# Attention and quantized feed-forward on one core: later reciprocals' halves, mixed pieces kept as integers, a calendar of weight jobs

## The chip, the cores and the metric

One Trainium2 chip, one of its cores. The metric is device time in microseconds of one launch; the time shown is the median of three runs. The profile is of one execution of the program.

Engines by the profile's names: PE (matrix products), PEld (its loading of the stationary operand), DVE (vector engine), ACT (scalar engine), POOL, and SP, whose queue (SPq) issues nearly all transfers. Each engine and SP's queue work through their own instructions in order; semaphores make one wait for another.

## The reference

All of it is in fp32: x is 16 x 512 x 512 (16 batch elements of 512 tokens), the context 16 x 120 x 512.

```python
x = x + attention(layernorm(x), ctx, ctx, Wq, Wk, Wv, Wo)    # 16 heads of 32, rotary positions on q and k
h = act_qdq(layernorm(x))
up   = act_qdq(h @ lpbq_dequant(w_up).T)       # 512 -> 1536
gate = act_qdq(h @ lpbq_dequant(w_gate).T)
gate = act_qdq(gate * u16(sigmoid(gate)))
x = x + act_qdq(gate * up) @ lpbq_dequant(w_down).T
```

`act_qdq` rounds a whole tensor to 16 bits with one scale, the tensor's largest absolute value over 32767. So gate, its product with the sigmoid, up, and the last product each need a maximum over all 16 elements before any of their values can be quantized. `lpbq_dequant` rounds weights to 4 bits in blocks of 32.

## The kernel before

Tokens are handled one batch element after another; a step of 512 tokens is one column block of PE. There are four stages.

**Attention** (L176 to L660). For each element `b` a loop runs over four slots `g` = 0 to 3, each with four heads. While element `b` is here, element `b+1` (`nxt`) has its queries made, `b-1` (`old`) is divided by its sums, projected and added to x, and `b-2` (`older`) is normalized and its largest absolute value found. A slot holds, in this order: scores of PE; DVE's maxima over keys (L335), turned by PE (L347, tile `tm`) and made into negated maxima `nm` (L354); the rotation of new queries on DVE (L217, L219) and POOL; values and sums of the slot before; exponentials. In slot 0 `old.reciprocals` makes 1/sum on DVE (L394), a copy to fp32r on ACT (L488), and then on DVE, in place, the lower halves of half the rows (L489, `two_halves`), which the copy must precede. The copy's tile `rh` shares its buffer with a raw weight, so it also waits for that weight's store. In slot 1 `old.divide` spreads the reciprocals over the heads by a matmul (L400, `rp`) and multiplies (L404). Three PSUM banks of tag `w` serve `qp`, `tm`, `pv`, `rp`, `op` and the rest in turn. In elements with `b % 4` in 1 to 3, up to 11, the slots 0 and 1 also hold parts of the next group's keys (`kvs.go_on`); elements 4, 8 and 12 to 15 have none.

**Gate** (L765 to L963). Tokens are quantized to int16, transposed by a DMA, and split into fp32r pieces: `hi` by POOL or DVE (L732), `lo` (L735) and `mix` = hi - 4096 lo by DVE (L738). An element has six chunks `f`, each two blocks of 128 gate columns; chunk `i` runs in `step(i)`: the mixed products of chunk `i+1` (`begin`, 8 matmuls), ACT's copy of chunk `i-1` out of PSUM and its store, ACT's division of `i+1` (L802), then the rest of `i` (16 matmuls). Then DVE finds the largest values of chunk `i-1` (L819, twice). Element `b+1` is quantized in the first step of `b` (third step for the first) and its pieces are made in steps 1 to 4. The same loop prepares the other weights: a block is loaded, quantized on DVE, turned by PE through two banks, cut into three parts and stored. Twelve blocks of up start at elements 1 to 12 and take one job per step; four blocks of down start in step 4 of elements 2, 5, 8 and 11, their six jobs one per step, beside those of up.

**Up** (L967 to L1155). The same steps with up's weights, elements 15 and 14 first (their pieces are still there), the others from their stored int16 tokens (`xq_d`, fetched into `xq`, two buffers). In each step a gate tile is loaded (`gt<-g_d`, seven buffers), turned by ACT (L980, L986) and DVE (L990, L991) into its product with the sigmoid, stored (`p_d<-gt`), and multiplied by up on POOL (L1014) for the largest product (L1018). Up itself is stored too (`u_d<-t_wu`, three buffers).

**Down** (L1157 to the end). The products are quantized, split and multiplied by down's weights.

PE, DVE and ACT, and in gate and up POOL too, follow the order of the code; SP's order is made by the scheduler of the language from its own estimate of when things are ready.

Of the kernel before, what the change touches and what calls it, by code (L numbers as in the profile page):

```python
# [53 lines left out]
def tile_xattn_ffn(  # L54
# [41 lines left out]
    xq_d = [dram.tile([P, NQ, ND, P], I16, name=f"xq_{b}") for b in range(B)]  # L96

# [84 lines left out]
    with ExitStack() as at:  # L182
# [92 lines left out]
        class Element:  # L275
# [66 lines left out]
            def maxima(self, g):  # L342
# [9 lines left out]
                hl = two_halves(p2.tile([P, DK], F32R, tag="mh", name=f"mh_{nm}"), mx, low_m)  # L352
# [36 lines left out]
            def reciprocals(self, part=slice(0, S)):  # L389
# [5 lines left out]
                two_halves(self.rh[:, part], self.rc[:, part], low_r, nc.scalar.copy)  # L395
# [90 lines left out]
        def two_halves(hl, t, low, copy=nc.vector.tensor_copy):  # L486

            copy(hl, t)  # L488
            nc.vector.scalar_tensor_tensor(  # L489
                out=hl, in0=hl.bitcast(F32), scalar=low, in1=t, op0=ALU.mult, op1=ALU.add  # L490
            )
            return hl
# [62 lines left out]
        for b in range(B):  # L555
# [8 lines left out]
            for g in range(NG):  # L564
# [13 lines left out]
                here.maxima(g)  # L578
                for f in rest:
                    f()  # L580
# [13 lines left out]
                if older and g in (1, 2):  # L594
                    for q in ((1,), (2, 3))[g - 1]:
# [43 lines left out]
        last.reciprocals(halves[0])  # L639
        for g in range(NG):  # L640
            last.divide(g, halves[0])
        last.reciprocals(halves[1])
        rest = last.output(0)
# [90 lines left out]
    def split_low(p, q):  # L734
        nc.vector.tensor_tensor(  # L735
            as_runs(p.lo, q), q, as_runs(p.hi, q).bitcast(F32), ALU.subtract
        )
        nc.vector.scalar_tensor_tensor(  # L738
# [27 lines left out]
    with ExitStack() as gu:  # L766
# [5 lines left out]
        class Tokens:  # L772


            def __init__(self, b, nm):
                self.b, self.nm, self.p = b, f"{nm}_{b}", []
                self.q = xpool.tile([P, NQ, ND, P], I16, tag="xq", name=f"xq_{self.nm}", bufs=2)
# [5 lines left out]
            def low(self, d):  # L783
                split_low(self.p[d], self.q[:, :, d, :])
# [67 lines left out]
        def quantize(b):  # L852
# [6 lines left out]
            nc.sync.dma_start(xq_d[b], xs[b].q)  # L859
# [64 lines left out]
        ups, downs = [], []  # L924
        for b in range(B):
            for f in range(N2):
                i = b * N2 + f

                def middle():
                    if f == (0 if b else 2) and b + 1 < B:  # L930
                        quantize(b + 1)

                def after():

                    if b == 0:
                        high = {3: ((0, nc.vector), (1, nc.gpsimd), (2, nc.gpsimd)), 4: ((3, nc.vector),)}
                        low = {3: (0,), 4: (1, 2, 3)}
# [492 lines left out]
```

## Time and profile before

| | us |
|---|---|
| median of three runs (range) | 2675.11 (2673.24 to 2676.17) |
| profiled execution: time / span | 2674.77 / 2673.0 |
| PE busy, share of the span | 2518.4, 94% |
| DVE / POOL / ACT busy | 2107.2 / 1598.2 / 1101.5 |
| mean granted clock of PE | 0.976 |
| HBM traffic over the span | 178 GB/s |

Attention lasts to 954 us, gate to 1526, up to 2080, and down begins at 2118 (its first matmuls) and runs undisturbed from 2148. The page's slices show PE near full everywhere but at the changes of stage; what PE loses inside a stage is in short gaps, which only its timeline shows. In a timeline row the columns are the start, the length, engine, line, operation with its tiles, and in brackets the idle time before it and what ended that.

### The profile page before, as it was taken

The numbers are of one execution on the slowest core, as the hardware profiler recorded it, in microseconds if no ns is written. First come the engines' busy times: TensorE is split into PE (matmuls) and PEld (weight loads), VectorE is DVE, ScalarE is ACT, GpSimd is POOL, SyncE is SP. The second block draws the span as 40 slices with busy tenths as digits, with TensorE's granted clock in tenths as the row PEclk, the third lists the DMA queues.
The fourth block names the chain that finished last, engine by engine and source line by source line (L and its number), as shares of the span: only waits on it lengthen the run. The fifth ranks groups of instructions, "written<-read, shape, count | busy, mean of one in ns | idle before, by whom it ended". The sixth has DMA issues, their size and how long they took to land. (4 is left out here: it accounts for less than half of the span.)

```text
span 2673.0 us, 30019 instructions
## 1 busy us (share of the span) xinstructions
PE 2518.4 (94%) x10610; PEld 1674.4 (63%) x10610; DVE 2107.2 (79%) x2889; ACT 1101.5 (41%) x1199; POOL 1598.2 (60%) x1011
## 2 busy tenths in 40 slices
PE   8899999999999779999999999999999489999999
PEld 4344334344333258778787878877777368888887
DVE  4677877887787657887886589999998778888886
ACT  1222222232222224444444377776667344444442
POOL 4467656565754345555554157776665467777775
PEclk9999999999999889999999999999999699999999
DMA  4011221121110076766665788888888877777774
GB/s 157 19 63 48 75 78 48 52 75 51 59 57 24 24 267 201 224 201 205 218 192 178 270 289 286 282 286 270 285 278 282 333 252 252 252 252 252 252 252 142
DMA packets 264399, 486.83 MB, mean 182 GB/s; under 512 B 47024, under 2 KB 65584, under 8 KB 264240
## 3 DMA queue, kind: packets, MB, share of 16 engines
q1 hardware_dynamic: 264080, 484.31, 53.4%
q8 instruction: 84, 1.38, 0.2%
q14 instruction: 75, 0.61, 0.1%
q0 software_dynamic: 160, 0.52, 0.0%
HBM read 255.66 MB, written 221.25 MB: 178 GB/s over the span
## 5 line engine op out<-in xcount | busy, mean ns | idle before, releaser
L732 POOL TENSOR_SCALAR oh_d<-oq_d 128x512 fp32r<-128x512 int16 x190 | 398.9, 2121 | 153.1 <-DVE oq_d L1220 153.1
L1014 POOL TENSOR_TENSOR po<-gt,t_wu 128x1024 f32<-128x1024 f32 x96 | 231.5, 2411 | 241.9 <-DVE gt L991 145.1
L308 PE MATMUL qp<-xnT,wq_sb 128*128 128x512 f32 x512 | 237.6, 607 | 2.3 <-ACT cT L204 2.3
L410 PE MATMUL op<-wo_sb,ao 128*128 128x512 f32 x512 | 233.9, 605 | 0.2 <-DVE ao L404 0.2
L387 ACT COPY ao<-pv 128x512 f32<-128x512 f32 x64 | 37.5, 586 | 467.8 <-PE pv L378 467.8
L819 DVE TENSOR_REDUCE max_g<-t_wg 128x1 f32<-128x1024 f32 x96 | 116.7, 1216 | 133.5 <-ACT t_wg L814 133.5
L732 POOL TENSOR_SCALAR xh_g<-xq_g 128x512 fp32r<-128x512 int16 x60 | 122.3, 2058 | 163.5 <-DMA xq_g<-xi 157.7
L796 PE MATMUL mm_wg<-xm_g,wg 128*128 128x512 f32 x768 | 202.5, 406 | 9.4 <-DMA wg<-wg_d 4.6
L1237 PE MATMUL dn_d<-wd,om_d 128*128 128x512 f32 x768 | 194.7, 403 | 17.6 <-DMA wd<-wd_d 6.4
L752 PE MATMUL mm_wg<-xl_g,wg 128*128 128x512 f32 x768 | 207.5, 392 | 0.0
L752 PE MATMUL mm_wg<-xh_g,wg 128*128 128x512 f32 x768 | 206.2, 390 | 0.0
L220 POOL TENSOR_TENSOR rt_q<-rt_q,sin_q 128x512 f32<-128x512 f32 x64 | 81.3, 1270 | 192.9 <-DVE rt_q L217 192.9
L1220 DVE SCALAR_TENSOR_TENSOR oq_d<-pq_d,r_o,uq_d 128x1024 int16<-128x1024 int16 x96 | 127.5, 1328 | 82.1 <-ACT uq_d L1173 82.1
L752 PE MATMUL mm_wu<-xl_u,wu 128*128 128x512 f32 x672 | 184.7, 397 | 2.1 <-ACT mm_wu L802 2.1
L1237 PE MATMUL dn_d<-wd,ol_d 128*128 128x512 f32 x768 | 184.6, 389 | 0.4 <-ACT dn_d L1249 0.4
L796 PE MATMUL mm_wu<-xm_u,wu 128*128 128x512 f32 x672 | 172.6, 397 | 12.7 <-ACT t_wu L814 6.5
L1237 PE MATMUL dn_d<-wd,oh_d 128*128 128x512 f32 x768 | 184.5, 389 | 0.0
L1237 PEld LDWEIGHTS dn_d<-wd,om_d 128*128 128x128 f32 x768 | 144.9, 192 | 62.2 <-DVE om_d L738 18.9
L752 PE MATMUL mm_wu<-xh_u,wu 128*128 128x512 f32 x672 | 180.0, 390 | 0.0
L308 PEld LDWEIGHTS qp<-xnT,wq_sb 128*128 128x128 f32 x512 | 92.6, 190 | 133.7 <-issue 104.6
L796 PEld LDWEIGHTS mm_wg<-xm_g,wg 128*128 128x128 f32 x768 | 147.8, 196 | 43.0 <-DVE xm_g L738 8.5
L814 ACT COPY t_wg<-mm_wg 128x1024 f32<-128x1024 f32 x96 | 97.2, 1012 | 173.5 <-PE mm_wg L752 138.3
(254 smaller groups left out, 5602.1 us busy)
## 6 DMA issues: line engine op xcount, KB each, us to landing
g_d<-t_wg SPq DMA_DIRECT2D x96, 512.0 KB, 3.7
gt<-g_d SPq DMA_DIRECT2D x96, 512.0 KB, 4.6
u_d<-t_wu SPq DMA_DIRECT2D x96, 512.0 KB, 5.8
p_d<-gt SPq DMA_DIRECT2D x96, 512.0 KB, 5.1
p<-p_d SPq DMA_DIRECT2D x96, 512.0 KB, 4.8
u<-u_d SPq DMA_DIRECT2D x96, 512.0 KB, 5.8
xt<-in_x_dram SPq DMA_DIRECT2D x16, 1024.0 KB, 5.3
x<-xt SPq DMA_DIRECT2D x16, 1024.0 KB, 4.3
```

Of the source, the lines that this page charges most:

```text
L220: nc.gpsimd.tensor_tensor(v(t), v(t), sin, ALU.mult)
L308: nc.tensor.matmul(ps, lhsT=wq_sb[:, d, ts(g, P)], rhs=self.xnT[:, d, :], start=(d == 0), stop=(d == ND - 1),)
L387: nc.scalar.copy(self.ao[:, g, :], pv)
L410: nc.tensor.matmul(ps, lhsT=self.ao[:, g, ts(q, P)], rhs=wo_sb[:, g, :], start=(g == 0), stop=(g == NG - 1),)
L732: engine.tensor_scalar(as_runs(p.hi, q), q, TO_256, TO_256, ALU.add, ALU.subtract)
L752: nc.tensor.matmul(ps[:, j, :], lhsT=lhs(j, i)[k], rhs=rhs(j, i)[k], start=(k == 0 and i == 0), stop=(k != 1 and i == n - 1), skip_group_c ...
L796: nc.tensor.matmul(self.ps[:, j, :], lhsT=lhs(j, d), rhs=self.x.p[d].mix, start=(d == 0), stop=(d == ND - 1), skip_group_check=True,)
L814: nc.scalar.copy(self.t, halves(self.ps))
L819: nc.vector.tensor_reduce(maxes[:, i : i + 1], self.t, AX.XYZ, ALU.max, **how)
L1014: nc.gpsimd.tensor_tensor(flat(g.po), flat(g.tile), flat(c.t), ALU.mult)
L1220: nc.vector.scalar_tensor_tensor(out=oq.rearrange("p f t -> p (f t)"), in0=pq, scalar=r_o, in1=uq, op0=ALU.mult, op1=ALU.mult,)
L1237: nc.tensor.matmul(self.ps[j], lhsT=self.p[f // 2].all()[k][:, f % 2, ts(j, P)], rhs=wd.made[f][k], start=(k == 0 and f == 0), stop=(k != ...
```

## The change

Five edits. (1) The lower halves of the reciprocals become a step of their own (`lower_reciprocals`), called in slot 1 after the maxima of the next element's scores; the quotients of the first two head groups move ahead of the key work of slot 1, the other two stay behind it; the three remaining maxima of normalized rows all stand in slot 2. (2) In gate the mixed pieces of elements 0 to 13 are turned into int16 by ACT (they are multiples of 256) in steps 2 and 3 and stored in `xn_d`. In up they are fetched beside the tokens, and ACT makes the fp32r piece again; DVE's L738 is left out there. The token tiles `xq` have one buffer rather than two; the store of tokens is a job of its own (`keep`) and left out for elements 14 and 15. (3) The weight jobs follow a calendar by step number. (4) The second element is quantized in step 1 of the first, and its lower pieces are made in pairs. (5) The scale of the largest gate is found at step 2 of up instead of 3. The first number after a job's start in the calendar is a step of the block's element, counted from 0; for down, 4 is the fifth step of its element and 7 to 10 are steps 1 to 4 of the next.

```diff
...
+    xn_d = [dram.tile([P, ND, S], I16, name=f"xn_{b}") for b in range(B)]
...
                 nc.vector.reciprocal(self.rc[:, part], self.sm[:, part])
-                two_halves(self.rh[:, part], self.rc[:, part], low_r, nc.scalar.copy)
+                nc.scalar.copy(self.rh[:, part], self.rc[:, part])
+            def lower_reciprocals(self, part=slice(0, S)):
+                lower_half(self.rh[:, part], self.rc[:, part], low_r)
...
-        def two_halves(hl, t, low, copy=nc.vector.tensor_copy):
-
-            copy(hl, t)
+        def lower_half(hl, t, low):
             nc.vector.scalar_tensor_tensor(
                 out=hl, in0=hl.bitcast(F32), scalar=low, in1=t, op0=ALU.mult, op1=ALU.add
             )
-            return hl
...
                 here.maxima(g)
+                if g == 1 and old:
+                    old.lower_reciprocals()
                 for f in rest:
                     f()
...
                     older.largest(0)
                     older.end_normalize(3)
-                if older and g in (1, 2):
-                    for q in ((1,), (2, 3))[g - 1]:
+                if older and g == 2:
+                    for q in range(1, NQ):
                         older.largest(q)
                 if new and g == 2:
                     for q in range(NQ):
...
                         old.reciprocals()
                     if nxt:
                         nxt.query(1)()
+                if g == 1 and old:
+                    for i in range(2):
+                        old.divide(i)
                 if g < 2 and kvs:
                     kvs.go_on(2)
                 if g == 1 and old:
-                    for i in range(NG):
+                    for i in range(2, NG):
                         old.divide(i)
                 if g == 2 and old:
                     for q in range(2):
...
         engine.tensor_scalar(as_runs(p.hi, q), q, TO_256, TO_256, ALU.add, ALU.subtract)
-    def split_low(p, q):
+    def split_low(p, q, mix=True):
         nc.vector.tensor_tensor(
             as_runs(p.lo, q), q, as_runs(p.hi, q).bitcast(F32), ALU.subtract
         )
+        if mix:
+            split_mix(p)
+    def split_mix(p):
         nc.vector.scalar_tensor_tensor(
             out=p.mix, in0=p.lo.bitcast(F32), scalar=-SPLIT, in1=p.hi.bitcast(F32),
...
             def __init__(self, b, nm):
                 self.b, self.nm, self.p = b, f"{nm}_{b}", []
-                self.q = xpool.tile([P, NQ, ND, P], I16, tag="xq", name=f"xq_{self.nm}", bufs=2)
+                self.q = xpool.tile([P, NQ, ND, P], I16, tag="xq", name=f"xq_{self.nm}", bufs=1)
             def high(self, d, engine):
                 self.p.append(Pieces(xpool, "x", [P, S], 8, f"{self.nm}_{d}"))
                 split_high(self.p[d], self.q[:, :, d, :], engine)
-            def low(self, d):
-                split_low(self.p[d], self.q[:, :, d, :])
+            def low(self, d, mix=True):
+                split_low(self.p[d], self.q[:, :, d, :], mix)
+            def keep(self):
+                nc.sync.dma_start(xq_d[self.b], self.q)
+            def short_mixes(self, pool, ds):
+                if ds[0] == 0:
+                    self.n = pool.tile([P, ND, S], I16, tag="xn", name=f"xn_{self.nm}", bufs=1)
+                for d in ds:
+                    nc.scalar.mul(self.n[:, d, :], self.p[d].mix.bitcast(F32), 1.0 / 256.0)
+                if ds[-1] == ND - 1:
+                    nc.sync.dma_start(xn_d[self.b], self.n)
+            def fetch(self):
+                nc.sync.dma_start(self.q, xq_d[self.b])
+                self.n = xpool.tile([P, ND, S], I16, tag="xn", name=f"xn_{self.nm}", bufs=1)
+                nc.sync.dma_start(self.n, xn_d[self.b])
+            def mix(self, d):
+                nc.scalar.mul(self.p[d].mix, self.n[:, d, :], 256.0)
         class Chunk:
             def __init__(self, w, x, b, f):
...
                 xi, xs[b].x1.rearrange("p q d -> p (q d)"), AF.Copy, scale=r_x
             )
             nc.sync.dma_start_transpose(xs[b].q.rearrange("p q d t -> p (q d) t"), xi)
-            nc.sync.dma_start(xq_d[b], xs[b].q)
         def up_weight(o):
...
         for d in range(ND):
             xs[0].high(d, nc.vector if d < 2 else nc.gpsimd)
             xs[0].low(d)
+        xs[0].keep()
         load(1)
         normalize(1)
         wg.load(range(4, NF))
-        nc.sync.dma_start(xq_d[0], xs[0].q)
         nc.vector.tensor_scalar(s_xw, s_x, WHOLE, None, ALU.mult)
         order = [B - 1, B - 2, *range(B - 2)]
...
         chunks[0].x = xs[0]
         chunks[0].begin()
         chunks[0].divide()
-        ups, downs = [], []
+        jobs = {}
+        for o in range(NF):
+            start = (o + 1) * N2
+            when = ((1, 2, 4, 5), (0, 1, 3, 4), (0, 1, 4, 5))[o % 3]
+            for j, job in zip(when, up_weight(o)):
+                jobs.setdefault(start + j, []).append(job)
+        for o in range(ND):
+            start = (3 * o + 2) * N2
+            for j, job in zip((4, 5, 7, 8, 9, 10), down_weight(o)):
+                jobs.setdefault(start + j, []).insert(0, job)
         for b in range(B):
             for f in range(N2):
                 i = b * N2 + f
                 def middle():
-                    if f == (0 if b else 2) and b + 1 < B:
+                    if f == (0 if b else 1) and b + 1 < B:
                         quantize(b + 1)
+                    if f in (2, 3) and b < B - 2:
+                        xs[b].short_mixes(wp, ((0, 1), (2, 3))[f - 2])
                 def after():
                     if b == 0:
                         high = {3: ((0, nc.vector), (1, nc.gpsimd), (2, nc.gpsimd)), 4: ((3, nc.vector),)}
-                        low = {3: (0,), 4: (1, 2, 3)}
+                        low = {3: (0, 1), 4: (2, 3)}
                     else:
                         high = {k: ((2 * k - 2, nc.gpsimd), (2 * k - 1, nc.gpsimd)) for k in (1, 2)}
                         low = {2: (0, 1), 3: (2,), 4: (3,)}
...
                     if i > 0:
                         chunks[i - 1].largest(max_g, **size)
                         chunks[i - 1].largest(top_g)
+                    for job in jobs.pop(i, ()):
+                        job()
+                    if f == 2 and b + 1 < B - 2:
+                        xs[b + 1].keep()
                     if f == 2 and b + 2 < B:
                         load(b + 2)
                     if f == 4 and b + 2 < B:
                         normalize(b + 2)
-                    if f == 0 and 1 <= b <= NF:
-                        ups.extend(up_weight(b - 1))
-                    if f == 4 and b % 3 == 2 and b < NF:
-                        downs.extend(down_weight(b // 3))
-                    for jobs in (downs, ups):
-                        if jobs:
-                            jobs.pop(0)()
                     if b == B - 1:
                         wu.load((0,) if f == 0 else (2 * f - 1, 2 * f))
...
             def middle():
                 for j in sig[k]:
                     gates[j].sigmoid2()
+                if splits:
+                    xu[order[n + 1]].mix(f)
             def after():
                 if k == 0:
                     wu.load((NF - 1,))
                 if splits:
-                    xu[order[n + 1]].low(f)
+                    xu[order[n + 1]].low(f, False)
                 if n + 2 < B and f == ND:
                     b = order[n + 2]
                     xu[b] = Tokens(b, "u")
-                    nc.sync.dma_start(xu[b].q, xq_d[b])
+                    xu[b].fetch()
                 if n == B - 1:
                     wd.load((0,) if f == 0 else range(max(1, 2 * f - 3), 2 * f - 1), (0,))
...
                 m_g = over_all([max_g, top_g], "g")
                 s_g, r_g = scale_of(m_g[:, 0:1], s_xw, "g")
                 nc.vector.tensor_tensor(r_g, r_g, s_xw, ALU.mult)
-            if k == 3:
+            if k == 2:
                 nc.vector.tensor_copy(m_p, m_g[:, 1:2])
...
```

More of the change, by code (lines that the diff above doesn't have):

```diff
@@ L351, in maxima @@
                 )
-                hl = two_halves(p2.tile([P, DK], F32R, tag="mh", name=f"mh_{nm}"), mx, low_m)
+                hl = p2.tile([P, DK], F32R, tag="mh", name=f"mh_{nm}")
+                nc.vector.tensor_copy(hl, mx)
+                lower_half(hl, mx, low_m)
                 t = p2.tile([P, NB, DK], F32R, tag="nm", name=f"nm_{nm}", bufs=1)
@@ L639, in tile_xattn_ffn @@
         last.reciprocals(halves[0])
+        last.lower_reciprocals(halves[0])
         for g in range(NG):
@@ L642, in tile_xattn_ffn @@
         last.reciprocals(halves[1])
+        last.lower_reciprocals(halves[1])
         rest = last.output(0)
```

## The prediction

> **What bounds the kernel now.** I read the page first (busy shares, then the slices), then busy time by stage, then PE's own timeline with the gaps in it, and for each gap the timeline of the engine or queue that ended it. The profiled execution took 2674.77 us (span 2673.0 and 1.8 around it); the median of the three runs is 2675.11, so a sum made on this execution stands 0.3 us below it.
>
> Busy time by stage (columns: stretch, its length, PE, PEld, DVE, ACT, POOL, granted clock, DMA share, GB/s); the rows are attention, gate, up in two parts, the change-over, and down:
>
> ```profile
> 0.00:954.00 954.00, 888.09 (x3593) 363.53 (x3593) 706.53 (x1329) 233.85 (x323) 539.68 (x523) 0.98 0.18 61
> 954.00:1526.00 572.00, 551.12 (x2410) 452.54 (x2411) 417.90 (x465) 236.22 (x232) 285.54 (x144) 0.97 0.68 218
> 1526.00:1755.00 229.00, 223.37 (x979) 182.71 (x978) 212.01 (x218) 163.26 (x162) 150.91 (x62) 1.00 0.85 286
> 1755.00:2080.00 325.00, 315.14 (x1320) 241.17 (x1319) 300.17 (x290) 224.64 (x223) 213.99 (x89) 1.00 0.84 284
> 2080.00:2148.00 68.00, 24.98 (x86) 18.19 (x85) 44.95 (x76) 20.97 (x22) 31.15 (x15) 0.66 0.76 283
> 2148.00:2673.00 525.00, 515.72 (x2229) 416.22 (x2227) 425.60 (x514) 222.51 (x241) 376.94 (x180) 1.00 0.69 242
> ```
>
> PE leads in every stage, so the change is worth what it takes out of PE's gaps, and no more. On PE's timeline an undisturbed chunk of gate or up takes 5.44 us from start to start, so an element of six takes 32.64. Three kinds of gap matter.
>
> Attention, element 4, slot 1, both counted from 0 (timelines of DVE, PE): DVE idles 1.85 us for ACT's copy of the upper halves, then makes the lower ones, and the transposed maxima reach PE 2.42 us late.
>
> ```profile
> 280.23 3.34 DVE L394 RECIPROCAL rc<-sm 128x512 f32<-128x512 f32 x1
> 285.42 0.75 DVE L489 SCALAR_TENSOR_TENSOR rh<-rh,low_r,rc 128x512 fp32r<-128x512 f32 x1 [1.85 <-ACT rh L488]
> 287.31 2.37 DVE L335 TRANSPOSE_TENSOR_REDUCE mt<-st 128x32 f32<-128x1024 f32 x2
> 289.97 0.33 PE L347 MATMUL tm<-ident,mt 128*128 128x128 f32 x1 [2.42 <-DVE mt L340]
> ```
>
> Gate, element 3: the up weight is transposed in the step that also turns the third part of a down weight. The two banks are full, and PE waits until DVE has read the second part:
>
> ```profile
> 1088.13 0.69 DVE L169 TENSOR_TENSOR wt_wd<-tp_wd,wt_wd 128x512 f32<-128x512 f32 x1
> 1088.92 1.09 PE L159 MATMUL tp_wu<-ident,wt_wu 128*128 128x128 f32 x4 [3.73 <-issue]
> ```
>
> Up (waits of SP's queue, then its timeline, then issues with time to landing and DVE's groups, all between 1820 and 2050): each load of a gate tile waits until the store of the previous tenant of its buffer, issued just before, has landed. Store, landing, load, next store: the stores of products go out every 5.88 us (69 of them from 1665.9 to 2071.7), slower than 5.44.
>
> ```profile
> SPq L1002 <- DMA p_d<-gt: 143.9, 39, 4.8
> ...
> 1908.05 0.57 SPq L1002 DMA_DIRECT2D gt<-g_d  x1
> 1908.71 0.56 SPq L1009 DMA_DIRECT2D p_d<-gt  x1
> 1909.32 0.62 SPq L815 DMA_DIRECT2D u_d<-t_wu  x1
> 1913.92 0.57 SPq L1002 DMA_DIRECT2D gt<-g_d  x1
> ...
> p_d<-gt SPq DMA_DIRECT2D x39, 512.0 KB, 5.2
> ...
> L738 DVE SCALAR_TENSOR_TENSOR xm_u<-xl_u,xh_u 128x512 fp32r<-128x512 f32 x25 | 22.2, 888 | 0.9
> ```
>
> **The change, part by part.**
>
> *Lower halves, maxima, quotients (attention).* DVE in slot 0 loses 0.75 and the wait of 1.85, together 2.60. The same gap of 2.41 to 2.42 stands in elements 4, 8, 12 and 13 (289.97, 512.84, 735.48, 786.46), all without key work, with 1.42 in 14 (835.98). In 15 (881.10) the gap is 3.82, of which a wait of 0.69 and the 0.75 vanish, less 0.3 until the scores end: 1.1. Sum 4 x 2.42 + 1.42 + 1.1 = 12.2. The granted clock fell to half for 3.4 us at 736.7 and 787.9, right behind two of these gaps: 1.7 each, 3.4. Against it: in slot 1 the 0.75 now stands between the negated maxima and the rotation. PE ends the exponents' matmuls 0.66 after DVE's nm (380.23 to 380.89), the lower halves come after 0.75 + 0.22 of signal: 0.3 for the first quotient in 14 elements, 4. The quotient gaps now present (16, 11.5 in all) are bank waits; with two quotients ahead of the key work some go, and the later rotation makes others: I count 2 gained. The maxima (0.68 each) move from slot 1 to 2, where DVE idles 0.70 for an output matmul (421.33). Net 14; bounds 8 (no clock, no bank wait gained) and 18.
>
> Rule weighed: the Trainium skill, "TensorE: Matmul & The Clock Gate", part 1, has the clock fall after an idle window of about 3.4 us. Of four stalls of 2.42 us here two were followed by half clock; by the page's figure none need be, and the sum would be 3.4 less.
>
> *Calendar of weight jobs (gate).* Elements 3, 6, 9 and 12 take 39.74, 41.29, 40.21 and 40.46 us, the others with a weight 33.1 (32.64 and 0.46 for four transposes). Twelve more transposes cost 3 x 0.46, so 34.5 is their floor: 161.7 - 138.0 = 23.7. In the calendar no step turns both weights, and the down weight's first turn comes two steps after its quantization (6.9 on DVE, 1065.4 to 1072.3) rather than one. DVE's fullest step is step 2: lower halves and mixes 2.8, two maxima 2.4, rest of a turn 1.4, 6.6 in 5.44; a bank is needed again one step after. I take 22; bounds 15 (a stall of 2 left in each) and 24.
>
> *Mixed pieces as integers, write side.* Four ACT conversions in each of 14 elements, two in step 2 and two in step 3 (all steps counted from 0): bounded by the 0.62 of ACT's fp32r cast and the 0.71 of its int16 output from 128x512. ACT is busy 41% in gate, two conversions are 1.4 beside 2.0 of a step's own: hidden by that idle time. One store of 512 KB per element at 218 GB/s: hidden, since 354 GB/s is seen elsewhere (2050 to 2110); if not, a landing of 3.7 (the row of g_d) each, off PE's path. On SP it waits for ACT's last conversion and stands before a store of gate that ACT has yet to make; the tokens' own store, now its own job, is put by the scheduler where it was.
>
> *First tokens.* Stall before element 1: 2.74 + 0.96, and 6.8 us of half clock. The quantization one step earlier does little: SP issues 24 weight loads until 974.3, the transposition went out at 976.8 and can go about 1.4 sooner. 1.4; bounds 0 and 6.
>
> *Up, the mix on ACT.* DVE per element: six times 0.72 + 1.28 + 1.21 + 1.21 is 26.5, four lower halves of 1.02 are 4.1, four mixes of 0.89 are 3.6: 34.2 before, 30.6 after, against 32.64. ACT's step is 1.02 + 1.15 + 1.01 + 1.14 = 4.32 of 5.44; with 0.62 in four of six steps 4.94, so PE covers it with 0.5 to spare. What is late next is SP. The built order of the changed kernel has, per element, only four loads with no later product store between them and the one they wait for (six before); the other two stand behind a later one, and the two token fetches between stores without a load. Four cycles of 5.88 and about 5.9 for the two other steps are 29.4, under 32.64. Bytes: 20 transfers of 512 KB in 32.64 us are 321 GB/s against 279 now and 354 seen. From the start of element 2 (1587.1) to PE's last up matmul (2080.5) 493.4 us pass; 85 steps of 5.44 are 462.4. Of 31 I take 28, leaving 0.2 an element; bounds 5 (SP still at 5.88 from element 8 on) and 31.
>
> *One buffer of tokens instead of two.* A fetch now waits for the last reader of the buffer, the fourth lower half, in step 3; it goes out in step 4 and lands in 6.5, and POOL reads it at the next element's first step, 10.9 later. The product store behind it on SP waits for a later DVE operation anyway. Cost 0; if that cover is gone, up to 6.5 in each of 14. Rule weighed: the Trainium skill, "Trainium Kernel Development and Optimization", Best Practices, wants double buffering so that transfers overlap compute, which speaks against this edit; with every landing exposed the sum would be 91 worse. The two steps of distance in the order decide for me.
>
> *Scale of the largest gate a step earlier:* some ten DVE operations of 0.15 to 0.2, moved, not added: 0, at most 2 either way.
>
> *Change-over.* The last store of up went out at 2088.3, 7.8 after PE's last matmul, behind SP's lag and full output buffers. Without the lag up to 8 go; the loads of down weights and DVE's chain of small operations to 2112.9 stay. I take 4; bounds 0 and 8.
>
> Sum: 14 + 22 + 1.4 + 28 + 4 = 69.4, so 2674.8 - 69.4 = 2605.
>
> **Rivals.** *Up stays on SP's queue.* For: 512 KB more per element, and landings of products grew from 3.3 to 5.2 as traffic ran on; from 6.0 on the four cycles and the rest fill 32.64. Against: the order above. Gains lost 28 - 5 and about 3 of the change-over: 2631.
> *ACT becomes up's bound.* If each mix shows in full, 56 x 0.62 = 35, 2640. For: ACT works in order and its copies already waited 69 us for stores. Against: 0.5 spare a step.
> *The attention edit does nothing,* because the moved 0.75 is paid again in slot 1: 2619.
> *Slower.* The single token buffer holds the transposition in gate: an ordinary element's last mix is ready at 1058.3, PE wants it at 1061.8, so 3.5 of delay is free and the rest falls on PE. To pass 2675 all 14 elements must lose 5.0, a transposition 8.5 late each time. Against: its last reader is done two steps ahead.
>
> **How the numbers follow.** All parts work: 0.69, 2605, own range 2594 to 2618. Up on SP: 0.13. Attention nothing: 0.09. ACT: 0.05. Slower: 0.04. The range 2590 to 2633 takes in the first three. About 0.2% (5.3 us) is what a measurement can tell from no change; between the cases and that bound lies little: faster 0.95, same 0.01, slower 0.04.
>
> **What would show it.** Right: no idle at the transposed maxima in elements 4, 8, 12, 13; gate elements 3, 6, 9, 12 near 34.5; up elements near 32.7 to the end; product stores following their DVE operation within 3 us rather than 11.8. Wrong: SP's wait for landed products still near 3.7 a step, ACT rows in front of up's divisions, or POOL idle at the tokens' upper halves for longer than before.

## The result and the profile after

The changed kernel takes 2638.31 us (median of four, 2635.48 to 2643.51) against 2675.64 for the kernel before: ratio 0.9864, 95% interval 0.9846 to 0.9881. It is faster, by half of what was forecast: 37 us instead of 69, and above the range of 2590 to 2633.

Its profiled execution took 2643.51 (span 2641.7). Busy time by stage, the columns as before; the rows are attention, gate, and up in two parts:

```profile
0.00:946.00 946.00, 888.27 (x3593) 361.56 (x3593) 717.11 (x1329) 234.18 (x323) 538.79 (x523) 0.98 0.18 61
946.00:1516.00 570.00, 551.87 (x2408) 450.17 (x2409) 416.30 (x465) 262.74 (x287) 278.58 (x145) 0.97 0.71 230
1516.00:1745.00 229.00, 228.38 (x1009) 188.81 (x1008) 209.41 (x206) 182.51 (x193) 152.15 (x64) 1.00 0.91 316
1745.00:2049.00 304.00, 299.98 (x1290) 238.73 (x1289) 281.55 (x246) 233.35 (x248) 199.36 (x86) 1.00 0.88 306
```

PE's share of attention and of up's first part has grown. Gate's row has hardly changed: 551.87 of 570 us busy, where it was 551.12 of 572. For exact borders I take PE's own marks: the first mixed matmul of gate, the first of up, the last matmul of up, the first of down.

| us | before | after | gained | forecast |
|---|---|---|---|---|
| attention, to gate's first matmul | 954.4 | 946.7 | 7.7 | 14 |
| gate | 565.8 | 564.0 | 1.8 | 23.4 (22 and 1.4) |
| up | 560.3 | 539.3 | 21.0 | 28 |
| change-over | 37.4 | 36.9 | 0.5 | 4 |
| down | 555.1 | 554.9 | 0.2 | 0 |

The profiled execution was the slowest of the four. Most of the experiments below leave some stages as they are here. Over the profiles with the same work in a stage, attention ends at 945.7 on average (14 profiles, 940.8 to 949.8; with the old attention 954.1 in three), gate takes 561.7 (6, 560.4 to 564.0) and up 536.0 (9, 531.0 to 539.6). By these averages the gains are 8.4, 4.1 and 24.3, the 37 us of the medians.

**Attention**, the same slot of element 4, PE and DVE. The wait for ACT's copy is gone, and the 2.42 us in front of `tm` are down to 0.39. In their place PE waits 0.17 for the negated maxima and 0.43 for a bank that the rotation frees, now that the lower halves stand in front of the rotation:

```profile
285.71 3.35 DVE L397 RECIPROCAL rc<-sm 128x512 f32<-128x512 f32 x1
290.21 2.37 DVE L336 TRANSPOSE_TENSOR_REDUCE mt<-st 128x32 f32<-128x1024 f32 x2
295.64 0.74 DVE L494 SCALAR_TENSOR_TENSOR rh<-rh,low_r,rc 128x512 fp32r<-128x512 f32 x1
...
293.43 0.33 PE L348 MATMUL tm<-ident,mt 128*128 128x128 f32 x1 [0.39 <-DVE mt L341]
295.78 0.51 PE L365 MATMUL st<-nm,ones 32*128 32x512 f32 x4 [0.17 <-DVE nm L357]
297.67 1.09 PE L406 MATMUL rp<-rh,rep 128*128 128x512 f32 x2 [0.43 <-DVE ra_q L220]
```

**Gate.** The collision is gone: elements 3, 6, 9, 12 take 34.49, 34.38, 34.50, 34.38, within 0.2 of the forecast floor of 34.5, and the 15.8 us that PE spent at `tp_wu` are down to 1.8. But elements 5, 8, 11 and 14, which took 33.1 and 32.6, now take 38.48, 38.48, 39.62 and 34.85. PE's waits from 946 to 1510:

```profile
PE mm_wg L832 <- DVE xm_g L753: 15.1, 10, 2.8
PE mm_wg L832 <- DMA wg<-wg_d: 5.0, 2, 4.6
PE tp_wu L160 <- DVE wt_wu L152: 1.8, 3, 1.0
```

One such stall, ahead of element 5 and followed back through the timelines of PE, SP and POOL (element 4 starts its own work at 1094.3):

```profile
1127.54 0.73 PE L832 MATMUL mm_wg<-xm_g,wg 128*128 128x512 f32 x2 [2.85 <-DVE xm_g L753]
...
1103.01 0.32 SPq L898 DMA_DIRECT2D wu_d<-wa_wu  x1
...
1105.85 0.34 SPq L135 DMA_DIRECT2D wt_wu<-in_L_ffn_w_up_dram  x1
1106.28 3.01 SPq L894 DMA_TRANSPOSE xq_g<-xi  x1
...
1092.18 1.29 POOL L172 TENSOR_TENSOR wa_wd<-wt_wd,wt_wd 128x512 f32<-128x512 f32 x1 [3.59 <-ACT wt_wd L171]
1093.46 8.27 POOL L883 TENSOR_SCALAR x1t<-x1t,ln_mv,ln_rstd 128x512 f32<-128x512 f32 x4
```

Read from the bottom: the calendar puts the rest of the down weight's third turn into step 4, in front of the normalization of the tokens two elements on. POOL idles 3.59 us for it, then normalizes for 8.27. Only then can ACT quantize (it ends 9.5 after the element's start; before, 5.0), and only behind the up weight's stores and load does SP issue the transposition (12.0; before, 5.0). The fourth mix of the next tokens is ready at 33.2, where before it was at 24.9; PE begins with these tokens at 28.3 and stands for that mix from 30.4. Small losses stand beside this one in elements 4, 7 and 10 (33.9, 33.6 and 34.4, before 33.1).

**Up.** Counted from 0 in the order of up, all chunks of elements 1 to 9 take 5.44; from 10 on they take 5.4 to 6.8, because the old wait is back. SP's waits from 1820 to 2050 (us in all, times, longest), its timeline around a pair of token fetches (a row `x2` is two loads and the wait between them), the issues with their time to landing, and ACT's new group (busy time, mean ns of one, idle time in front); the last two are from 1820 to 2050 again:

```profile
SPq L1047 <- DMA p_d<-gt: 123.2, 35, 6.0
```

```profile
1737.22 0.55 SPq L1054 DMA_DIRECT2D p_d<-gt  x1
...
1738.75 1.03 SPq L815 DMA_DIRECT2D xq_u<-xq  x1
1739.88 1.05 SPq L817 DMA_DIRECT2D xn_u<-xn  x1
1741.02 0.55 SPq L1054 DMA_DIRECT2D p_d<-gt  x1
...
1743.26 0.97 SPq L1054 DMA_DIRECT2D p_d<-gt  x1
...
1747.94 5.54 SPq L1047 DMA_DIRECT2D gt<-g_d  x2
1753.58 0.56 SPq L1054 DMA_DIRECT2D p_d<-gt  x1
```

```profile
p_d<-gt SPq DMA_DIRECT2D x42, 512.0 KB, 5.3
```

```profile
L820 ACT ACTIVATE xm_u<-xn_u 128x512 fp32r<-128x512 int16 x23 | 14.2, 618 | 0.0
```

ACT's mix costs the 0.62 that was assumed, with no idle time in front. SP still stands 3.5 us at each of 35 loads, and product stores go out up to 12 us after the start of the DVE operation they follow.

### The profile page after: what moved, and what is told of

Read it like the earlier page. It is cut to its first block, busy times and chain, and to the rows that moved or that the text cites. A ratio compares the mean times of both kernels' runs of the same rounds, so it can differ in the third digit from the quotient of the medians.

```text
span 2641.7 us, 30187 instructions
## 1 busy us (share of the span) xinstructions
PE 2510.0 (95%) x10610; PEld 1674.0 (63%) x10610; DVE 2095.2 (79%) x2833; ACT 1155.9 (44%) x1311; POOL 1577.0 (60%) x1011
## 5 line engine op out<-in xcount | busy, mean ns | idle before, releaser
L336 DVE TRANSPOSE_TENSOR_REDUCE mt<-st 128x32 f32<-128x1024 f32 x128 | 151.7, 1223 | 30.2 <-PE st L330 29.9
```

The costliest lines, as they stand in the source:

```text
L336: nc.vector.tensor_reduce(self.mt[:, 2 * i : 2 * i + 2, 0, :], self.st[i].rearrange("p h (c j) -> p h c j", j=DK), AX.X, ALU.max, apply_tr ...
```

## The experiments

Ratios are against the kernel before, with their 95% intervals; where there is one run only, its time is given. Stage times are from the profiles.

### Is it the calendar, or the single token buffer?

**Old calendar.** The jobs of the weights as before, one a step and behind the normalization again, everything else as changed:

```
-                    for job in jobs.pop(i, ()):
-                        job()
+                    if f == 0 and 1 <= b <= NF:
+                        ups.extend(up_weight(b - 1))
+                    if f == 4 and b % 3 == 2 and b < NF:
+                        downs.extend(down_weight(b // 3))
+                    for jobs in (downs, ups):
+                        if jobs:
+                            jobs.pop(0)()
```

> Changed kernel with the weight jobs of gate as before: one job a step, those of the down weight ahead of those of the up weight. All else as changed, the single token buffer and the short mixes too. Theory A: the heavy elements 3, 6, 9, 12 are back at 39.7 to 41.3 (23.7 lost), the late transpositions are gone (elements 5, 8, 11, 14 near 33, 22 to 24 won): within 4 us of the changed kernel, 2634 to 2642. Theory B (single token buffer, whatever the calendar): the heavy elements come back and the stalls of 5, 8, 11, 14 stay: about 2660.

2640.69 us, 0.9868 (0.9847 to 0.9888): the calendar as written is worth little. Gate takes 565.4 here, 3.7 more than the average of the runs with the calendar, and the medians cannot be told apart. Elements 3, 6, 9, 12 are back at 39.7 to 41.4, elements 5, 8, 11, 14 at 33.1, 33.1, 33.1, 32.6. Transpositions start 5.0 after each element's start, with one token buffer. The rival of the single buffer falls.

**Normalization ahead of the jobs.**

```
+                    if f == 4 and b + 2 < B:
+                        normalize(b + 2)
                     for job in jobs.pop(i, ()):
                         job()
...
-                    if f == 4 and b + 2 < B:
-                        normalize(b + 2)
```

> Changed kernel with one order reversed: in gate's step 4 the normalization of the tokens two elements on is issued before the step's weight jobs instead of behind them. Theory A (the calendar put the rest of a down weight's third turn in front of the normalization on POOL, so that the quantization, the transposition behind it and the last mixes of elements 5, 8, 11 and 14 come late): the quantization in elements 4, 7, 10 ends 5.0 after the element's start instead of 9.3 to 9.8; SP's queue still holds the transposition behind the up weight's stores, until about 8.5 instead of 12; the third and fourth mixes are ready at about 26 and 29.7, needed at 28.3; the elements 5, 8, 11, 14 fall from 38.5, 38.5, 39.6, 34.9 to about 34.5, 34.5, 35, 33; gate 564 to about 548, the whole 2621 to 2626. Theory B (the single token buffer is what holds the transposition): nothing changes, 2638.

2644.03 us, 0.9889 (0.987 to 0.9908): no gain. The quantization ended at 5.0 to 5.2 as expected, so POOL's order did hold it. But the transposition went out at 13.4, 11.8 and 11.9: behind POOL stood another holder, and it is the load of the next up weight, which waits on SP until the stores of the last have landed. SP's waits from 1084 to 1104, and its timeline:

```profile
SPq L135 <- DMA wu_d<-wt_wu: 5.8, 1, 5.8
```

```profile
1101.71 0.34 SPq L135 DMA_DIRECT2D wt_wu<-in_L_ffn_w_up_dram  x1
1102.15 3.03 SPq L894 DMA_TRANSPOSE xq_g<-xi  x1
```

**Transposition from ACT's queue,** alone and with the edit before:

```
-            nc.sync.dma_start_transpose(xs[b].q.rearrange("p q d t -> p (q d) t"), xi)
+            nc.scalar.dma_start_transpose(xs[b].q.rearrange("p q d t -> p (q d) t"), xi)
```

> Changed kernel with the tokens' transposition of gate issued from ACT's queue, right behind the quantization that it waits for, instead of from SP's queue. Theory A: in elements 4, 7, 10 it starts when the quantization ends, 9.3 to 9.8 after the element's start instead of 11.7 to 12.4, so each of the stalls in elements 5, 8, 11 falls by 2 to 3 us and nothing else moves: 2629 to 2633. Theory A with SP's queue as the main cause: the stalls go, 2618. Theory B (single token buffer): the transposition starts no earlier, 2638. Against all: 15 issues of 1.3 to 3 us in ACT's order may delay its divisions; ACT is 46% busy in gate, so I expect none of that.

> Both edits of the two runs before together. Theory A: quantization ends and transposition starts 5.0 after the start in every element, the mixes are ready near 24 to 26 of 28 needed; no element of gate above 34.5; gate 564 to about 541, the whole about 2615 (2612 to 2619). Theory B (single token buffer): 2638.

2693.43 us, 1.0085 (1.0052 to 1.0119), and 2687.34, 1.0047 (1.003 to 1.0065): slower than the kernel before, against both theories. The transposition now starts as soon as the quantization ends, but it takes twice as long to land. Issues between 987 and 1510, first of the changed kernel, then of the first of these two, and that one's longest wait of PE in gate:

```profile
xq_g<-xi SPq DMA_TRANSPOSE x14, 4.3
```

```profile
xq_g<-xi ACTq DMA_TRANSPOSE x14, 8.3
```

```profile
PE mm_wg L832 <- ACT t_wg L850: 31.0, 13, 5.7
```

ACT's copies out of PSUM are late as well, and PE waits for them. Why the transposition lands later from ACT's queue, no run shows.

**The up weight's load from ACT's queue** (elements 1, 4, 7, 10), then **the down weight's load too**. ACT keeps the order of the code, SP's is made by the scheduler:

```
-            nc.sync.dma_start(self.wt, self.w[ts(self.o, P), :])
+            (nc.scalar if self.tag == "wu" and self.o % 3 == 0 else nc.sync).dma_start(self.wt, self.w[ts(self.o, P), :])
```

```
-            nc.sync.dma_start(self.wt, self.w[ts(self.o, P), :])
+            (nc.scalar if self.tag == "wd" or self.tag == "wu" and self.o % 3 == 0 else nc.sync).dma_start(self.wt, self.w[ts(self.o, P), :])
```

> The normalization ahead of the weight jobs as in the first run, and the up weight's load in elements 1, 4, 7, 10 issued from ACT's queue in step 1, so that SP's queue no longer stands at that load until the stores of the previous up weight have landed (5.8 us in the first run) with the transposition behind it. Theory A2 (two holders, one behind the other: POOL's order for the quantization, SP's order for the transposition): in elements 4, 7, 10 the quantization ends 5.0 and the transposition starts 6 to 7.5 after the element's start, the last mixes are ready at 28 to 29 of 28.3 needed, the stalls of 2.85 us in elements 5, 8, 11 are gone or under 1; gate 564 to 542 to 547; the whole 2615 to 2624. Rival (the transposition is held by its one token buffer): no change against the first run, 2638 to 2644.

> As the run with the normalization ahead and the up weight's load on ACT's queue, and the down weight's load (768 KB) from ACT's queue too, at its own place in step 4 of elements 2, 5, 8 instead of where SP's order had pulled it, between the last down store and the up weight's stores of elements 3, 6, 9. Theory A3 (third holder: the bytes queued in front; in the run before, the transposition was issued at 6.7 to 7.2 but its issue took 5.7 to 6.8 instead of 1.8, behind 2.5 MB): 0.8 MB less in front is 2.5 us at 320 GB/s; the transposition's issue takes 3 to 4, POOL's first upper half starts at 12.5 to 13.5 instead of 15.6 to 17.2, the last mixes are ready at 29 to 30; the stalls in elements 5, 8, 11 fall from 5.4 to 0 to 2; gate 558 to 543 to 549, the whole 2620 to 2630. If bytes are not what holds it, gate stays at 558 and the whole at 2636.

The first: 2635.96 us, 0.985 (0.9833 to 0.9866), a miss. The transposition is issued at 7.2, 6.7 and 7.1 but its issue takes 6.8, 5.8 and 5.7 us, behind the 2.5 MB that were issued in the 5 us in front of it. The second, without the 768 KB of the down weight there: 2626.15 us, 0.9818 (0.9786 to 0.985), gate 547.7, elements 5, 8, 11 at 35.4, 35.0, 35.0. The same issue in element 4, first of the one, then of the other:

```profile
1100.48 6.82 SPq L894 DMA_TRANSPOSE xq_g<-xi  x1
```

```profile
1103.66 4.57 SPq L894 DMA_TRANSPOSE xq_g<-xi  x1
```

**The last 2 us: VectorE's order.** Both runs have the edits so far and up's gate loads on ACT's queue as well; that combination by itself is the last experiment on up, and what these two are to be compared with (gate 544.2, 2615.45 us). First the up weight's quantization behind the last two mixes, then ahead of the first two:

```
-            when = ((1, 2, 4, 5), (0, 1, 3, 4), (0, 1, 4, 5))[o % 3]
+            when = ((1, 3, 4, 5), (0, 1, 3, 4), (0, 1, 4, 5))[o % 3]
...
-                        low = {2: (0, 1), 3: (2,), 4: (3,)}
+                        low = {2: (0, 1), 3: (2, 3)} if b % 3 == 1 else {2: (0, 1), 3: (2,), 4: (3,)}
```

```
+                    if f == 2 and b % 3 == 1:
+                        for job in jobs.pop(i, ()):
+                            job()
                     if b + 1 < B:
                         for d, engine in high.get(f, ()):
```

> As the run before, and in elements 1, 4, 7, 10 the last two mixes of the next tokens come in step 3, ahead of the up weight's quantization (2.96 us on VectorE), which moves from step 2 to step 3. If what is left in elements 5, 8, 11 (2.0 to 2.3 each) is VectorE's order, the last mix is ready near 25 instead of 30.6 to 31.0 and these elements take 33.1 to 33.3: gate 541 to 543, the whole 2606 to 2612. If not, as the run before; if the later quantization holds the turn in step 4, its transposes wait 1 to 3 us in elements 4, 7, 10 and the gain is lost again.

> As the run with gate and weight loads on ACT's queue, and in elements 1, 4, 7, 10 VectorE quantizes the up weight ahead of the lower halves and mixes of step 2 instead of behind them: it has nothing to do from 9 to 16 us after the element's start, and the load, issued at 7.5, should have landed by 13 to 16. If the last 2 us in elements 5, 8, 11 are VectorE's order: the third and fourth mixes are ready near 24 and 27.5 instead of 27 and 30.6, elements 5, 8, 11 take 33.1 to 33.6, gate 538 to 541, the whole 2606 to 2612. If the load lands later than 16, the mixes are as late as before or later: 2614 to 2620.

Behind: 2623.21 us, 0.9808 (0.9794 to 0.9822). The mixes are ready at 24 to 26, and PE waits for the quantized weight instead, as the last sentence of the expectation has it. Its waits in gate:

```profile
PE tp_wu L160 <- DVE wt_wu L152: 10.0, 3, 4.0
```

Ahead: 2608.81 us, 0.9741 (0.9724 to 0.9758). Elements 5, 8, 11 take 33.24, 33.23, 33.23, elements 3, 6, 9, 12 34.4 to 34.5, gate 541.7; it is the fastest of all. The chain of element 4, in us after its start:

| kernel | quantized | transposition | first upper half | fourth mix | gate |
|---|---|---|---|---|---|
| changed | 9.5 | 12.0 | 16.5 | 33.2 | 564.0 |
| normalization first | 5.2 | 13.4 | 17.9 | 34.6 | 562.4 |
| and up weight's load on ACT | 5.2 | 7.2 | 17.2 | 33.8 | 558.1 |
| and down weight's load on ACT | 5.5 | 6.7 | 14.3 | 31.0 | 547.7 |
| and quantization ahead of mixes | 5.2 | 6.5 | 14.3 | 28.1 | 541.7 |

### What gave the gain in up?

**Without the integer mixes,** and **without their fetch alone:**

```
-                if splits:
-                    xu[order[n + 1]].mix(f)
...
-                    xu[order[n + 1]].low(f, False)
+                    xu[order[n + 1]].low(f)
```

```
-                self.n = xpool.tile([P, ND, S], I16, tag="xn", name=f"xn_{self.nm}", bufs=1)
-                nc.sync.dma_start(self.n, xn_d[self.b])
...
-                nc.scalar.mul(self.p[d].mix, self.n[:, d, :], 256.0)
+                nc.scalar.mul(as_runs(self.p[d].mix, self.q[:, :, d, :]), self.q[:, :, d, :], 256.0)
```

(the first also leaves out the conversions in gate, their store and their fetch; the second makes the pieces from the tokens' integers, so it leaves out the right values)

> Changed kernel without the mixed pieces as integers: no short mixes made, stored or fetched, VectorE makes all mixes in up as before. If the write side costs nothing (the prediction's zero), gate stays at 564; up returns to 34.2 an element at least, 560 in all as in the kernel before, the whole 2659. If the extra stores and the ACT conversions cost something in gate, gate is shorter than 564 by that. If the fetch of 512 KB an element is what fills the queue late in up, product stores lag less than before the edit.

> Changed kernel without the fetch of the short mixes in up: ACT makes the mixed pieces from the tokens' integers instead, the same instruction on another source, so the output is wrong and 512 KB an element less come in. Theory D (bytes: 20 transfers of 512 KB an element at a DMA share of 0.9): with 19 the landings shorten, the lag of the product stores stays under 6 us, no element of up over 32.64 but the last, up 530 to 532. Theory C (SP's order alone): the fetch step falls from 10 us of SP's time to about 6, an element's cycle on SP from 34.4 to about 30.5, and the same comes out; what tells them apart is the landing of a product store between 1720 and 2045: 5.3 as now under C, below 4.8 under D. Gate is as in the changed kernel, so the whole is 2627 to 2634.

Without the mixes: one run, 2666.88 us; up 559.7 as before the change, gate 564.9, so their write side costs nothing that can be seen. Without the fetch: 2680.36 us, 1.0017 (1.0004 to 1.003), up 574.0: fewer bytes, the mix still on ACT, and all of up's gain lost. Neither theory had this. SP's waits from 1720 to 2045:

```profile
SPq L1045 <- DMA p_d<-gt: 211.5, 53, 5.3
```

What the two share is SP's order as built (p, u: stores; g: gate load, gk needs the landing of the store p(k-7); x, n: token fetches):

```
changed        p34 u35 g41 p35 u36 g42 p36 u37 g43 p37 u38 x n p38 u39 g44 p39 u40 g45 g46
without fetch  p34 u35 g41 p35 u36 g42 p36 u37 g43 p37 u38 g44 x p38 u39 g45 p39 u40 g46
```

Of the 78 loads of tiles 12 to 89, those with no other product store between them and the one they wait for number 42 in the changed kernel, 72 before, 75 without the mixes, 73 without the fetch. With the second fetch the scheduler places loads behind a later store, and I take that to be how it helped. No run changed the order alone, and without the fetch one thing more is new: ACT, now a reader of the tokens, waits for their landing nine times, 9.2 us in all.

**Gate load a step later in the code.**

```
-                for j in range(3):
+                for j in range(2):
                     gate_load(j)
-            gate_load(k + 3)
+            gate_load(k + 2)
```

> Changed kernel with up's load of a gate tile issued one step later (tile k+2 in step k instead of k+3), so that the store it waits for was issued a step earlier; same buffers, same bytes. Theory C (what is left in up is SP's order: load waits for the landing of a product store just issued): all elements of up 1 to 14 at 32.64, the product stores within 3 us of DVE's operation to the end, the lag at the change-over gone; 7 us from the elements 10 to 14 and 1 to 5 from the last element and the change-over: 2625 to 2631. Theory D (the transfers themselves are full: 20 of 512 KB in 32.64 us, DMA share 0.9): the lag comes back from element 10 on and nothing changes, 2638.

2638.36 us, 0.9865 (0.9848 to 0.9881): nothing, and no test, for the scheduler put the loads back where their buffers come free; SP's order again has 42 of 78 right behind their store. Its up of 530.5 lies at the lower end of those of the unchanged code (531.0 to 539.6).

**Gate loads from ACT's queue,** in the changed kernel and in the kernel before:

```
-                nc.sync.dma_start(gt, part(g_d, c.b, c.f))
+                nc.scalar.dma_start(gt, part(g_d, c.b, c.f))
```

> Changed kernel with up's loads of gate tiles issued from ACT's queue at their place in the program, behind ACT's work of the step; product stores, u stores and token fetches stay on SP's. The run before with the load a step later in the program did not test this, since SP's order put the loads back right behind the stores that free their buffers. Theory C (SP's order: a load that waits for a landing holds the next product store): product stores follow DVE within 3 us to the end, up 530 instead of 539, the whole 2629 to 2634 for a gate of 564. Theory D (the transfers are full): the stores land later and later all the same, lags of 8 to 12 us or ACT waiting for the landings, up 535 to 545. Against both: 0.55 us of issue in each ACT step of 4.3 to 4.9, so ACT comes to 5.4 in four of six steps, and each of its waits would now show on PE: then up grows to 545 to 560.

> The kernel before the change, with one edit: up's loads of gate tiles are issued from ACT's queue. VectorE makes the mixes in up as it did. Theory E (VectorE's step, as predicted: 34.2 us an element against 32.64, so it is the next bound): 14 elements lose 1.56 each, up 546 to 552 instead of 560, the whole 2662 to 2668. Theory F (SP's order was the only bound of up, and the mix on ACT bought nothing but its effect on that order): up 527 to 533, the whole 2641 to 2648.

In the changed kernel: 2626.95 us, 0.9832 (0.9806 to 0.9858); up 527.4, every chunk from the second element on 5.44. From there on product stores go out 1.3 to 1.7 us after the start of their DVE operation, and up to 4.6 only in the last two elements. SP now waits for DVE instead of landings (1720 to 2045):

```profile
SPq L1054 <- DVE gt L1036: 194.1, 54, 4.5
```

Stores land in 3.8 us instead of 5.3 at 324 GB/s (1720 to 2030), more than the 303 of the changed kernel (1720 to 2045), so the transfers were not full. In the kernel before: 2654.12 us, 0.9922 (0.9907 to 0.9937); up 544.8, between the two theories but with the mark of the first, 33.45 an element and DVE full. Its row for 1720 to 2045, DVE 321.63 of 325:

```profile
1720.00:2045.00 325.00, 318.72 (x1393) 260.23 (x1392) 321.63 (x311) 234.63 (x231) 234.64 (x96) 1.00 0.90 298
```

So up had two bounds, one behind the other: SP's order to 545, DVE's step from there to 527. The mix on ACT takes away the second; of the first its fetch, by the reading above, took a part.

**Both loads and gate loads on ACT's queue,** with the normalization first:

> Changed kernel with the normalization ahead of the weight jobs, the two weight loads on ACT's queue and up's gate loads on ACT's queue. If the gains add: gate 548, up 527, the change-over 2 shorter as with the gate loads alone; 2612 to 2618.

2615.45 us, 0.9778 (0.9765 to 0.9792), gate 544.2, up 527.4: the gains add.

### Attention

**Old attention** (lower halves, quotients and second maximum back), and **the quotients alone back** behind the key work:

```
-                if g == 1 and old:
-                    for i in range(2):
-                        old.divide(i)
...
-                    for i in range(2, NG):
+                    for i in range(NG):
```

> Changed kernel with the attention edits undone (lower halves of the reciprocals right behind the reciprocals, all quotients behind the keys, second row maximum in the third slot back in the second). By my sum attention loses 14, gate's first mixed matmul at 960.5; by the comparison of the two profiles 7.7, at 954.4. I now expect 954.4 and 2646, with the four idle times of 2.42 at the transposed maxima back and the new ones of 0.43 behind the second quotient gone.

> Changed kernel with one part of the attention edit undone: all four quotients behind the key work again; the lower halves and maxima stay where the change has them. In elements without key work in the slot the order is the same and nothing changes. In the elements with it the idle time of 0.43 behind the second quotient (122.84, 179.92, 242.79, 347.32 and so on) goes; if the bank then comes late for the last quotients, 0.7 to 0.95 come back there, as before the change. Gate's first mixed matmul 944 to 950 either way, 2633 to 2643.

One run each, 2643.97 and 2644.14 us. Gate starts at 952.9 and 950.3. The start alone moves by 9 us from run to run, so I added up PE's idle time up to gate's first mixed matmul instead, by the matmul that follows or precedes it:

| idle of PE, us | before | changed | old attention | quotients back |
|---|---|---|---|---|
| ahead of `tm` | 24.7 | 13.9 | 24.4 | 13.9 |
| ahead of `rp` | 14.7 | 10.0 | 15.0 | 16.6 |
| behind `rp` | 0.2 | 4.0 | 0.2 | 0.2 |
| `st`, behind the sums | 0.1 | 4.4 | 0.1 | 2.7 |
| all other | 24.0 | 23.5 | 24.4 | 26.1 |
| sum | 63.7 | 55.8 | 64.0 | 59.4 |

Undoing the attention edits brings back 8.2, where the change had taken 7.9. Putting the quotients back costs 3.6 in one run; 2.6 of it stand under "all other", so I leave their place at 1 to 4.

## Why the prediction was wrong

The direction was right, and the size was off by 32 us. By the averages over the runs, 19 of them were lost in one step, in gate; the rest went in attention, up and the change-over, 4 to 6 us in each.

*Calendar, the step that failed: "In the calendar no step turns both weights", with "I take 22; bounds 15 and 24".* The first is true, and the 23.7 came in (24 measured in elements 3, 6, 9, 12). The sum counted this alone and put what the moved jobs cost the other elements at nothing: 22 were lost in elements that I held undisturbed, 19.4 in 5, 8, 11 and 14 and 2.5 in 4, 7 and 10. I followed PE's banks and DVE and did not follow POOL and SP past the moved jobs, where the rest of the third turn, now in step 4, comes ahead of the normalization. The rival's "single token buffer holds the transposition in gate" named the right victim, a late transposition, and the wrong holder. With POOL's order, the two loads and DVE's order put right, gate takes 541.7: 24 us, the forecast's gain, but from four edits that the change does not have.

*Up: 28 forecast, 21 in the profile, 24 over the runs.* The mechanism was half right. DVE's step, costed at 34.2, bounded up at 33.45 when nothing else did. SP's cycle was mis-sized: "Four cycles of 5.88 and about 5.9 for the two other steps are 29.4". The other two are 6.0 (stores at 1737.2, 1741.0, 1743.3), but one of the four takes 10.3, to 1753.6: its two loads wait one behind the other for the stores of 1741.0 and 1743.3, issued behind the two fetches, which land 6.9 and 9.6 us after their issue. From the fifth fetch on an element so takes SP 34 us. "Up stays on SP's queue" came true in part; the bytes it named count only through that wait, for with the loads on ACT's queue the same bytes leave every chunk from the second element on at 5.44.

*Attention: 14 forecast, 7.7 in the profile, 8.4 over the runs.* The gaps at `tm` gave 10.8 of 12.2. The waits that come instead, 8.1 behind the quotients and at the negated maxima, less 4.7 gained at the quotients, cost 3.4 where I had 4 less 2. The clock's 3.4 cannot be found. The two stretches of half clock at 736.7 and 787.9 are gone, but all half clock before gate fell only from 47.0 to 43.1 us in the profiled pair, and it lay between 31.4 and 57.3 in the other runs with this attention.

*Change-over: 4 forecast, 0.5.* The last product store follows PE's last matmul by 9.1 before (the 7.8 of the prediction is the last store of up itself), 8.3 after and still by 7.0 to 8.2 in the runs with gate loads on ACT's queue, where SP hardly lags: most of it is not SP's lag but the work of ACT and DVE that ends up's last chunk.

*First tokens: 1.4 forecast, 0.* Elements 0 and 1 take 74.4 both times. *Write side and largest gate: 0, as forecast. The single token buffer: 0*, against the Trainium skill, "Trainium Kernel Development and Optimization", Best Practices, as weighed. The other rule weighed, "TensorE: Matmul & The Clock Gate", part 1, with its idle window of about 3.4 us: in gate half clock followed the waits of 2.85 at 1127.54 and 2.84 at 1234.03, so a shorter wait than the page's window sufficed here, and the measurement decides.

## What to carry to other kernels

When a job is moved to another step, list what it passes on every queue, the issuing engine's and POOL's too, and ask of each who waits behind it; a collision taken away in one element came back two elements on, through four engines. A queue whose order a scheduler makes is not moved by moving the code: put the transfer that waits for a landing on an engine whose order is yours, and measure it, for the transposition that was moved in the same way cost 55 us. And take bounds away one at a time before believing which edit paid: here the fetch seems to have helped by the order that came with it as well as by its data.

## What was not expected of the hardware

A transposing transfer issued from ACT's queue beside SP's traffic landed in 8.3 us instead of 4.3, and the kernel lost 55 us. On SP, the issue of the same transfer took 1.3 to 6.8 us, longest with most bytes in front. The half clock granted in attention differed by 26 us between kernels with the same attention code, and the start of gate by 9. Why up without the fetch is 14 us slower than before the change, with nearly the same order of loads, stays open.
